# Values of six attention units computed two units at a time, in a one-core cross-attention block

## The chip, the cores and the metric

The kernel runs on one NeuronCore of a Trainium2 chip. The core has five engines that run at the same time and meet only at semaphores: TensorE (PE, the matrix array; PEld is its weight load), VectorE (DVE), ScalarE (ACT), GpSimd (POOL) and SyncE (SP), which here only issues transfers. Matrix products land in PSUM, eight banks of 128 x 512 float32; everything else lies in SBUF. The metric is the device time of one execution, the median of several runs. All data is float32.

## The reference, cut to what matters

Four sequences (batch `B = 4`) of 512 tokens with 512 channels each attend, with 16 heads of 32 channels, to 512 context tokens of their own; a two-layer MLP with 2048 hidden channels follows.

```python
x = layer_norm(hidden_states, ln1_w, ln1_b)
q = (x @ q_w + q_b);  k = (ctx @ k_w + k_b);  v = (ctx @ v_w + v_b)   # heads of 32
scores = einsum('bhqd,bhkd->bhqk', q, k) / sqrt(32), masked
out = softmax(scores) @ v
hidden = out @ cproj_w + cproj_b + hidden_states
y = gelu(layer_norm(hidden, ln2_w, ln2_b) @ fc_w + fc_b) @ proj_w + proj_b
return hidden + y
```

The change touches only the order in which parts of `q`, `k`, `v` and of the first layer norm are computed, and how the products for `v` are cut. No number of the reference is left out or changed.

## The kernel before, in words

**Units and blocks.** The attention is cut into 16 units, numbered `w`: batch `w // 4`, group `w % 4` of four heads (128 channels). Each unit has two halves of 256 queries, so there are 32 blocks, numbered `p = 2 w + half`; a half is also called a pair in the code. A block (`block`, L349) issues the scores of eight tiles (two query tiles by four heads, `scores`, L324), which fill all eight PSUM banks, then takes each score tile through VectorE (`soften`, L335: add the mask, take the minimum) and ScalarE (L339: exponential and row sum), turns the results by 32 x 32 blocks on VectorE (`turn`, L347), takes the reciprocal of the sums (L366), spreads it on ScalarE into `rr` (L368) and turns that too (L372). What comes out is the tile `tb`.

**Exchange.** The turned blocks must change partition groups. `exchange` and `copies` (L390, L397) move `tb` to a tile `pT` or `gt`: four diagonal pieces are copied by GpSimd (L405), twelve others go by transfers on SP's queue (L410). A pair's move is issued only when its target is free. Pairs 0, 2, 4, 6, 8 share the target `pT` and pairs 1, 3, 5, 7 the target `gt`, so that the move of pair 2 is issued when pair 0 has been attended, at the start of block 3.

**Attend.** `attend` (L415) multiplies the exchanged probabilities with the unit's `v` (L429) and scales the result on VectorE into `oT` (L434). In blocks 3 to 8 a block begins with the attend of the pair three blocks back, followed at once by the next exchange, if one waits: block 3 attends pair 0, block 4 pair 1, block 5 pair 2 and so on.

**Dense items.** Between the scores and the next attend TensorE does dense work from a list per block, `put(p, ...)`: `prep_k(w)` (L257), `prep_q(w)` (L267) and `prep_v(w)` (L279). Each makes one PSUM tile of 128 x 512. For K and Q the stationary operand is a weight block of 128 x 128 and the moving one has 512 columns. For V it is turned round: a token block of the context is stationary and the weight block of one unit, 128 columns, moves; 16 matmuls make a tile, in the profile 32 instructions at L285 (each float32 matmul is two). ScalarE copies the tile to `v` (L290) and GpSimd adds the bias (`v_bias`, L321). `prep_v_pair(w)` (L300) exists already and serves units 10 to 15: the two units' weight blocks, neighbours in SBUF, move together as 256 columns (L310); two PSUM tiles come out, each holding two token blocks of both units, so ScalarE makes four copies of 128 x 256 (L314). Each item ends by issuing on SP the load of a later unit's weights into the place it has read: K and Q of unit `w + 2` (up to unit 9), V of unit `w + 2`. Such a load waits until the item's matmuls are done, and SP is in order.

**Where an item lands.** Each entry of a list has a cost; `block` calls `fill(0)` after the last `soften`, `fill(1)` after the `rr` work and `fill(2)` after the call of `exchange`.

```python
def run(work, budget=None):
    spent = 0.0
    while work and (budget is None or spent + work[0][0] / 2 <= budget):
```

`fill(0)` and `fill(1)` have a budget of `CHAIN = 3.4`, the cost of one item, `fill(2)` has none. A `do(...)` entry costs 0.0 and goes with the item ahead of it; a `next_(...)` entry costs 0.01, does not fit behind an item, and goes to the next fill. A `V(w)` entry is a whole pair of units at the cost of one item. The order of issue is the order on each engine's queue: nothing is reordered later.

**Layer norm 1 of batch 1.** It is computed in the transposed layout: `load_raw(1)` (L200) loads the transposed input, `store_rn(1)` (L205) writes mean and scale per token to DRAM, `load_rn(1)` (L213) reads them back as two broadcast rows (tile `hid`), `ln1_rows` (L218) applies them on GpSimd, two operations of 128 x 512 for each of four chunks (L221), and `ln1_affine` (L223) applies weight and bias on ScalarE into `xT` (L225), which `prep_q(4)` reads. `load_enc(1)` (L180) loads batch 1's context over batch 0's, once unit 3's V has read it.

Of the kernel before, what the change touches and what calls it, by code (L numbers as in the profile page):

```python
# [25 lines left out]
ND = D // P  # L26
# [27 lines left out]
def xattn_block(ctx: ExitStack, tc: tile.TileContext, x, rawT, encT, mask, q_w, k_w, v_w, c_w, fc_w, p_w, vecs, rows, out):  # L54
# [41 lines left out]
    def k_q(w, i):  # L96
        n = w % 4 * 2 + i
        return pbt[:, n * D : (n + 1) * D]
# [23 lines left out]
    def acc_tile(name):  # L122
        n = count[5]
        count[5] += len(banks) > 1
        return banks[n // 4 % len(banks)].tile([P, D], F32, tag="acc", name=name)
# [51 lines left out]
    def queue(b):  # L177
        return Q[0] if b else nc.sync

    def load_enc(b):  # L180
        for d in range(ND):
            queue(b).dma_start(out=eT[:, d, :], in_=encT[b, ts(d, P), :])
# [17 lines left out]
    def load_raw(b):  # L200
        S["xn", b] = [tiles.tile([P, L], F32, tag="xn", name=f"raw_{b}_{d}") for d in range(ND)]
        for d in range(ND):
            nc.sync.dma_start(out=S["xn", b][d], in_=rawT[b, ts(d, P), :])

    def store_rn(b):  # L205
        nc.vector.transpose(rnT, rn)
        d = S["rn", b] = dram.tile([2, L], F32, tag=f"rn{b}", name=f"rn{b}")
        for i in range(NI):
            nc.sync.dma_start(
                out=d.rearrange("a (t i q) -> i (a t) q", i=NI, q=HD)[i], in_=rnT[i * HD : i * HD + 2 * NT, :]  # L210
            )

    def load_rn(b):  # L213
        S["rows", b] = [hid2[:, i] for i in range(2)]
        for i in range(2):
            nc.sync.dma_start(out=S["rows", b][i], in_=S["rn", b][i : i + 1, :].broadcast_to([P, L]))

    def ln1_rows(b, *ds):  # L218
        for d in ds:
            for i, op in enumerate((ALU.mult, ALU.add)):  # L220
                nc.gpsimd.tensor_tensor(S["xn", b][d], S["xn", b][d], S["rows", b][i], op)  # L221

    def ln1_affine(b):  # L223
        for d in range(ND):
            nc.scalar.activation(  # L225
                xT[:, d, :], S["xn", b][d], AF.Identity,
                bias=vec[:, LN1B + d : LN1B + d + 1], scale=vec[:, LN1W + d : LN1W + d + 1],
            )
# [14 lines left out]
    def load_w(w, queue=None, names=("wk", "wq", "wv")):  # L243

        if w >= NW:
            return
        g = w % NG
        for i, (n, src) in enumerate((("wk", k_w), ("wq", q_w), ("wv", v_w))):
            if n in names:
                S[n, w] = kqv_w(w, i)  # L250
                (queue or Q[0]).dma_start(out=S[n, w], in_=src[:, g, :, :])

    def next_w(w, name):
        if w != SINGLE - 1:
            load_w(w + (2 if w < SINGLE else 1), names=(name,))
# [11 lines left out]
    def prep_q(w):  # L267
        b, g = divmod(w, NG)
        qT = k_q(w, 1)
        parts = [slice(0, L)] if w else [slice(0, 2 * P), slice(2 * P, L)]  # L270
        for c in parts:
            acc = acc_tile(f"accq_{w}_{c.start}")[:, c]
            for d in range(ND):
                nc.tensor.matmul(acc, S["wq", w][:, d, :], xT[:, d, c], start=(d == 0), stop=(d == ND - 1))  # L274
            nc.scalar.activation(qT[:, c], acc, AF.Identity, bias=qb[:, g : g + 1], scale=-scale)
        next_w(w, "wq")
        S["qT", w] = qT

    def prep_v(w):  # L279
        b = w // NG  # L280
        v = five.tile([P, NT, P], F32, tag="v", name=f"v_{w}")
        acc = acc_tile(f"accv_{w}")
        for t in range(NT):
            for d in range(ND):
                nc.tensor.matmul(  # L285
                    acc[:, ts(t, P)], eT[:, d, ts(t, P)], S["wv", w][:, d, :],
                    start=(d == 0), stop=(d == ND - 1),
                )
        load_w(w + 2, names=("wv",))
        nc.scalar.copy(v, acc.rearrange("p (t f) -> p t f", t=NT))  # L290
        S["v", w] = v
        if w:
            v_bias(w)
# [6 lines left out]
    def prep_v_pair(w, later=False):  # L300
        pair = range(w, w + 2)
        for u in pair:
            S["v", u] = five.tile([P, NT, P], F32, tag="v", name=f"v_{u}")
        n = 10
        wv = ptt[:, n * D : (n + 2) * D].rearrange("p (g d f) -> p d g f", g=2, d=ND)
        for i in range(2):
            acc = acc_tile(f"accv_{w}_{i}").rearrange("p (t g f) -> p t g f", t=2, g=2)
            for t in range(2):
                for d in range(ND):
                    nc.tensor.matmul(  # L310
                        acc[:, t], eT[:, d, ts(2 * i + t, P)], wv[:, d], start=(d == 0), stop=(d == ND - 1)
                    )
            for g, u in enumerate(pair):
                nc.scalar.copy(S["v", u][:, 2 * i : 2 * i + 2], acc[:, :, g])  # L314
        for u in pair:
            load_w(u + 2, names=("wv",))
            (held_back.append if later else run_)(lambda u=u: v_bias(u))

    def v_bias(w):
        v, bias = S["v", w], row[:, 2, ts(w % NG, P)]  # L320
        nc.gpsimd.tensor_tensor(v, v, bias[:, None, :].broadcast_to([P, NT, P]), ALU.add)  # L321
# [141 lines left out]
    def c_bias(b):  # L463
        for t in range(NT):
            add_row(S["h", b, t], 0)
# [650 lines left out]
    CHAIN, TURN = 3.4, 0.5  # L1116

    def do(fn):
        return [(0.0, fn)]

    def next_(fn):
        return [(0.01, fn)]

    def A(w):
        if w >= NW:
            return []
        return [
            (CHAIN, lambda: prep_k(w)),
            (CHAIN, lambda: prep_q(w)),
            (CHAIN, lambda: prep_v(w)),  # L1130
        ]

    def V(w, later=False):
        return [(CHAIN, lambda: prep_v_pair(w, later))]

    def C(b):
        return [(CHAIN, lambda t=t: cproj(b, t)) for t in range(NT)]
# [4 lines left out]
    def turns2(b):  # L1142
        return [(TURN, lambda d=d: ln2_turn(b, d)) for d in range(ND)]

    def inputs(b):
        ln = [(0.0, lambda part=part: ln1(b, part)) for part in range(3)]
        return do(lambda: load_x(b)), ln, turns1(b), do(lambda: load_enc(b))
# [70 lines left out]
    def cb(b):  # L1218
        return do(lambda: c_bias(b))
# [7 lines left out]
    def stat(b, *ts_):  # L1227
        return do(lambda: [stat2(b, t) for t in ts_])
# [6 lines left out]
    def put(p, *work, before=(), mid=()):  # L1235

        work = [item for part in work for item in part]
        ahead[p], mids[p] = list(before), list(mid)
        fills[p] = work

    k2, q2, v2 = A(2)
    k3, q3, v3 = A(3)
    k4, q4, v4 = A(4)
    k5, q5, v5 = A(5)
    k6, q6, v6 = A(6)
    put(0, [(CHAIN, lambda: prep_v(1)), v2], do(lambda: (load_raw(1), store_rn(1))), [k2])
    put(1, [k3, (0.0, lambda: prep_q(1)), (CHAIN, lambda: (prep_v(3), load_enc(1)))], next_(lambda: load_rn(1)))
    put(2, [q2], [q3], do(lambda: ln1_rows(1, 0, 1)))
    put(3, [k4], do(lambda: ln1_rows(1, 2, 3)), [v4])
    put(4, [k5, v5], do(lambda: ln1_affine(1)))  # L1250
    put(5, [q4, q5])
    put(6, [k6, q6])
    x1, x2, x3, x4 = inputs(2)
    k, q, v = A(7)
    c, t2 = C(0), turns2(0)
    put(7, [v6, k], cb(0))
    put(8, x1, [q, v], x4)
    put(9, c[:1], do(lambda: attend(3, 1)), x2[:2], c[1:2], x2[2:], stat(0, 0), c[2:3], stat(0, 1),
        c[3:], stat(0, 2), x3, stat(0, 3), rs(0))
    k, q, v = A(8)  # L1260
    put(10, [k], norm(0, 0, 1), [v], norm(0, 2, 3), do(fc_sums), [q], t2)
    k, q, v = A(9)
    put(11, [k, v], some(2), pb_(0), mid=do(lambda: y_sums(0)))

    x1, x2, x3, x4 = inputs(3)
    put(12, [q], some(2))
    k, q, v = A(10)
# [4 lines left out]
    k, q, v = A(11)  # L1272
    put(16, do(lambda: ln1_rows(3, *range(ND))), [k, q], some(2), h_(1, 0, 1))
    put(17, next_(lambda: ln1_affine(3)), h_(1, 2, 3), x4, cb(1), C(1))
    k, q, v = A(12)
    put(18, [q], some(2), pre(0, 1))
    k12 = k
    k, q, v = A(13)
# [3 lines left out]
    k, q, v = A(14)  # L1282
# [100 lines left out]
```

## Time and profile before

| | |
|---|---|
| Time, median of 3 runs | 755.8 us (755.66 to 756.85) |
| The profiled execution | 756.21 us, its span 754.4 us |
| TensorE busy | 749.5 us, 99% of the span |
| VectorE busy | 617.5 us, 82% |
| GpSimd busy | 403.6 us, 53% |
| ScalarE busy | 341.1 us, 45% |

The span is the part of the execution that the profiler's records cover; 1.8 us lie around it. A busy share is a mean over stages; the change lies in the first 125 us, where the attention is densest. The chain of work that ended last is read backwards from the end of the kernel: whoever is on it sets the time.

### The profile page before, as it was taken

Reading aid. Unit: us, or ns where it says so; the run is one execution under the profiler, and the core shown is the slowest. Engines: PE = TensorE matmul, PEld = TensorE weight load, DVE = VectorE, ACT = ScalarE, POOL = GpSimd, SP = SyncE. Lnnn points to the kernel's source line nnn. Section 1 sums busy time; section 2 is a strip of 40 time slices with the busy share of each in tenths; the row PEclk is TensorE's granted clock in tenths of the full one; section 3 lists DMA queues with packets and bytes.
Section 4 is the critical chain, followed back from the end, with each engine's and each line's share of the span. In section 5 each row is a group of like instructions: output and inputs, shape, how many; then the busy total and the mean of one; then the engine's idle time right before and its main releaser. Section 6 shows DMA issues by size and latency. Waiting matters only on the chain.

```text
span 754.4 us, 13326 instructions
## 1 busy us (share of the span) xinstructions
PE 749.5 (99%) x4514; PEld 536.4 (71%) x4514; DVE 617.5 (82%) x1225; ACT 341.1 (45%) x776; POOL 403.6 (53%) x401
## 2 busy tenths in 40 slices
PE   9999999999999999999999999999999999999998
PEld 6655555467667546575655776468888899988998
DVE  3889999879998779877987999949877986957865
ACT  2566776555884575648853578401302221021200
POOL 1436838358597987667869974532150014403153
PEclk9999999999999999999999999999999999999999
DMA  9988888466787797666756757766734402045001
GB/s 327 342 240 238 227 216 248 116 182 188 216 240 233 210 258 188 165 191 160 196 127 202 192 145 240 185 216 236 242 104 151 156 15 91 29 157 207 1 15 43
DMA packets 61124, 134.62 MB, mean 178 GB/s; under 512 B 11344, under 2 KB 17360, under 8 KB 60928
## 3 DMA queue, kind: packets, MB, share of 16 engines
q1 hardware_dynamic: 58736, 127.39, 58.7%
q0 software_dynamic: 1600, 5.97, 2.5%
q8 instruction: 36, 0.59, 0.3%
q10 hardware_dynamic: 720, 0.41, 0.2%
q14 instruction: 32, 0.26, 0.1%
HBM read 69.23 MB, written 11.02 MB: 106 GB/s over the span
## 4 chain that ended last, share of the span: by engine, by line
PE 99%; DVE 0%; issue 0%; POOL 0%; POOLq 0%; DVEq 0%
PE q L671 26%; PE r L912 10%; PE sc L329 9%; PE av L429 8%; PE acck L262 8%; PE accq L274 7%; PE accc L471 6%; PE accv L285 5%; PE accp L766 4%; PE accv L310 3%; PE q1p L979 2%; PE tp L169 1%; PE q1j L785 1%; PE q3j L785 1%; PE q4j L785 1%; PE q6j L785 1%
## 5 line engine op out<-in xcount | busy, mean ns | idle before, releaser
L339 ACT ACTIVATE ptt<-ptt,mn 128x512 f32<-128x512 f32 x256 | 181.7, 711 | 140.2 <-DVE mn L335 140.2
L335 DVE CUSTOM_DVE_ANT_0 ptt<-sc,mb 128x512 f32<-128x512 f32 x256 | 160.6, 682 | 19.3 <-PE sc L329 19.3
L347 DVE STREAM_TRANSPOSE tb<-ptt 128x1024 f32<-128x1024 f32 x128 | 153.3, 1217 | 0.0
L405 POOL COPY pT<-tb 32x1088 f32<-32x1088 f32 x96 | 104.6, 1090 | 33.4 <-DVE oT L434 13.5
L671 PE MATMUL q<-yT,gt 128*128 128x256 f32 x320 | 78.9, 379 | 0.0
L692 ACT ACTIVATE ga<-ga,vec 128x512 f32<-128x512 f32 x40 | 26.7, 714 | 90.7 <-DVE ga L625 90.7
L329 PE MATMUL sc<-pbt 32*128 32x512 f32 x512 | 66.6, 615 | 0.0
L671 PEld LDWEIGHTS q<-yT,gt 128*128 128x128 f32 x320 | 60.7, 190 | 8.2
L671 PE MATMUL q<-ys,gt 128*128 128x256 f32 x240 | 61.6, 379 | 0.0
L262 PE MATMUL acck<-xe,ptt 128*128 128x512 f32 x128 | 59.7, 610 | 0.0
L274 PE MATMUL accq<-xe,ptt 128*128 128x512 f32 (+1 forms) x136 | 58.1, 573 | 0.0
L671 PEld LDWEIGHTS q<-ys,gt 128*128 128x128 f32 x240 | 45.6, 190 | 6.2
L625 DVE TENSOR_TENSOR ga<-q,ga 128x512 f32<-128x512 f32 (+1 forms) x60 | 36.2, 603 | 14.7 <-PE q L671 11.7
L339 ACT ACTIVATION_READ_ACCUMULATOR ptt<-ptt,mn 128x1 f32 x256 | 47.8, 187 | 0.0
L440 POOL TENSOR_TENSOR hid<-hid,row 128x512 f32<-128x512 f32 x18 | 24.0, 1359 | 42.7 <-DMA hid<-xa 42.6
L274 PEld LDWEIGHTS accq<-xe,ptt 128*128 128x128 f32 x136 | 25.0, 190 | 30.4 <-issue 23.0
L429 PE MATMUL av<-pT,v 128*32 128x256 f32 x768 | 46.4, 382 | 0.0
L262 PEld LDWEIGHTS acck<-xe,ptt 128*128 128x128 f32 x128 | 23.6, 194 | 31.9 <-issue 23.5
L329 PEld LDWEIGHTS sc<-pbt 32*128 32x128 f32 x512 | 27.5, 183 | 25.6 <-issue 16.9
L471 PE MATMUL accc<-wc,oT 128*128 128x512 f32 x96 | 42.5, 597 | 0.0
L285 PEld LDWEIGHTS accv<-ptt,xe 128*128 128x128 f32 x320 | 37.0, 192 | 4.9 <-DVE mn L335 2.7
L321 POOL TENSOR_TENSOR v<-v,row 128x512 f32<-128x512 f32 x16 | 20.3, 1278 | 37.2 <-ACT v L290 29.7
(263 smaller groups left out, 1436.8 us busy)
## 6 DMA issues: line engine op xcount, KB each, us to landing
pT<-tb SPq DMA_DIRECT2D x288, 136.0 KB
pbt<-p_w_dram SPq DMA_DIRECT2D x40, 256.0 KB
gt<-ws SPq DMA_DIRECT2D x20, 512.0 KB
gt<-tb SPq DMA_DIRECT2D x48, 136.0 KB
xe<-tb SPq DMA_DIRECT2D x48, 136.0 KB
pbt<-fc_w_dram SPq DMA_DIRECT2D x24, 256.0 KB
gt<-fc_w_dram SPq DMA_DIRECT2D x20, 256.0 KB
ptt<-k_w_dram SPq DMA_DIRECT2D x16, 256.0 KB
```

The lines of the kernel that those rows point to most:

```text
L262: nc.tensor.matmul(acc, S["wk", w][:, d, :], eT[:, d, :], start=(d == 0), stop=(d == ND - 1))
L274: nc.tensor.matmul(acc, S["wq", w][:, d, :], xT[:, d, c], start=(d == 0), stop=(d == ND - 1))
L285: nc.tensor.matmul(acc[:, ts(t, P)], eT[:, d, ts(t, P)], S["wv", w][:, d, :], start=(d == 0), stop=(d == ND - 1),)
L329: nc.tensor.matmul(S["sc", w, qt][h], qT[r, ts(qt, P)], kT[r, :], start=True, stop=True)
L335: nc.vector.tensor_tensor_reduce(out=s, in0=S["sc", w, qt][h], in1=S["mb", w // NG], scale=1.0, scalar=FMAX, op0=ALU.add, op1=ALU.min, acc ...
L339: nc.scalar.activation(s, s, AF.Exp, bias=mn, scale=-1.0, accum_out=S["sums", w][:, qt, h : h + 1])
L347: nc.vector.transpose(tv[:, qt % 2, 2 * k : 2 * k + 2], S["ps", w, qt, k])
L405: nc.gpsimd.tensor_copy(pT[ts(i, HD), i], tb[ts(i, HD), i])
L429: nc.tensor.matmul(av[ts(h, HD), : 2 * P].rearrange(shape, **kw), v[:, t, ts(h, HD)], p[t][h], start=(t == 0), stop=(t == NT - 1),)
L471: nc.tensor.matmul(acc, S["oT", b][:, g, ts(t, P)], wc[:, g, :], start=(g == 0), stop=(g == NG - 1))
L671: nc.tensor.matmul(o, x[:, k], y[:, k], start=(k == 0), stop=(k == 1))
L912: nc.tensor.matmul(r, x[:, c], w[:, c], start=(c == 0), stop=(c == NP // 2 - 1))
```

## The change

The lists of blocks 0 to 8 are written anew. V of units 2 and 3, of 4 and 5 and of 6 and 7 is made by `prep_v_pair`, in blocks 1, 4 and 8, in place of six single `prep_v` in blocks 0, 1, 3, 4, 7 and 8. K of units 3, 5 and Q of unit 7 move one block earlier into the freed places (K of unit 2 from the third to the second place of block 0). `ln1_rows(1)`, GpSimd's part of batch 1's layer norm 1, is issued whole at the end of block 2, where before half of it stood in block 2 and half in block 3; `ln1_affine(1)` stays in block 4, now in `fill(1)` without an item ahead of it.

```diff
-    put(0, [(CHAIN, lambda: prep_v(1)), v2], do(lambda: (load_raw(1), store_rn(1))), [k2])
-    put(1, [k3, (0.0, lambda: prep_q(1)), (CHAIN, lambda: (prep_v(3), load_enc(1)))], next_(lambda: load_rn(1)))
-    put(2, [q2], [q3], do(lambda: ln1_rows(1, 0, 1)))
-    put(3, [k4], do(lambda: ln1_rows(1, 2, 3)), [v4])
-    put(4, [k5, v5], do(lambda: ln1_affine(1)))
+    put(0, [(CHAIN, lambda: prep_v(1)), k2], do(lambda: (load_raw(1), store_rn(1))), [k3])
+    put(1, [(CHAIN, lambda: prep_q(1))], V(2), do(lambda: load_enc(1)), next_(lambda: load_rn(1)))
+    put(2, [q2], [q3], next_(lambda: ln1_rows(1, *range(ND))))
+    put(3, [k4], [k5])
+    put(4, V(4), next_(lambda: ln1_affine(1)))
     put(5, [q4, q5])
     put(6, [k6, q6])
     x1, x2, x3, x4 = inputs(2)
     k, q, v = A(7)
     c, t2 = C(0), turns2(0)
-    put(7, [v6, k], cb(0))
-    put(8, x1, [q, v], x4)
+    put(7, [k, q], cb(0))
+    put(8, x1, V(6), x4)
```

The function that the new lists call, unchanged by the diff:

```python
def prep_v_pair(w, later=False):
    pair = range(w, w + 2)
    ...
    for i in range(2):
        acc = acc_tile(f"accv_{w}_{i}").rearrange("p (t g f) -> p t g f", t=2, g=2)
        for t in range(2):
            for d in range(ND):
                nc.tensor.matmul(
                    acc[:, t], eT[:, d, ts(2 * i + t, P)], wv[:, d], start=(d == 0), stop=(d == ND - 1)
                )
        for g, u in enumerate(pair):
            nc.scalar.copy(S["v", u][:, 2 * i : 2 * i + 2], acc[:, :, g])
    for u in pair:
        load_w(u + 2, names=("wv",))
        (held_back.append if later else run_)(lambda u=u: v_bias(u))
```

## The prediction

> **What bounds the kernel now.** I read the page's head and its chain first, then the chain in order of time for the stretch that the change touches, then each other engine's timeline there.
>
> ```profile
> span 754.4 us, 13326 instructions
> PE 99%; DVE 0%; issue 0%; POOL 0%; POOLq 0%; DVEq 0%
> ```
>
> The chain never leaves TensorE: a microsecond taken from its list is taken from the end, unless a wait comes up. The chain in order of time (start, length, what; blocks 0, 1, 3, 4, 7, 8 in turn, then a pair of V, then two rows of later blocks):
>
> ```profile
> 24.22 7.34 PE accv L285 x64
> 31.57 3.44 PE acck L262 x8
> ...
> 36.93 3.63 PE acck L262 x8
> 40.56 3.43 PE accq L274 x8
> 43.99 3.57 PE accv L285 x32
> ...
> 60.35 3.63 PE acck L262 x8
> 63.98 3.57 PE accv L285 x32
> ...
> 71.35 3.63 PE acck L262 x8
> 74.98 3.57 PE accv L285 x32
> 78.55 1.86 PE av L429 x32
> 80.41 1.93 PE sc L329 x16
> ...
> 104.10 3.77 PE accv L285 x32
> 107.87 3.44 PE acck L262 x8
> ...
> 115.13 3.63 PE accq L274 x8
> 118.76 3.57 PE accv L285 x32
> ...
> 226.89 6.91 PE accv L310 x32
> ```
>
> ```profile
> 323.39 7.10 PE accv L310 x32
> ...
> 442.28 2.97 PE sc L329 x16
> ```
>
> The reader is to see that the pieces abut (71.35 + 3.63 = 74.98, + 3.57 = 78.55), so TensorE waits nowhere here, and that an item right behind scores costs 0.2 more than one behind another item: 3.63 against 3.43, 3.77 against 3.57, 7.10 against 6.91. VectorE, from block 4 into block 5:
>
> ```profile
> 80.02 0.40 DVE L372 STREAM_TRANSPOSE tb<-rr 128x256 f32<-128x256 f32 x1
> 80.48 0.42 DVE L434 TENSOR_TENSOR oT<-av,pT 128x256 f32<-128x256 f32 x1
> 81.50 0.69 DVE L335 CUSTOM_DVE_ANT_0 ptt<-sc,mb 128x512 f32<-128x512 f32 x1 [0.60 <-PE sc L329]
> ```
>
> VectorE ends a block only just when TensorE does (80.42 against 80.41) and then idles 0.60 until the first score tiles are there, 1.09 behind the start of the scores. That 0.60 is all its slack per block: the second engine near the bound.
>
> **The change, TensorE.** Each V pair replaces two singles; the rest is regrouped. By the rows above, dense time per block, before and after:
> - Block 0: 7.34 + 3.44 = 10.78; then V1, K2, K3 = 3.77 + 3.44 + 3.44 = 10.65. -0.13.
> - Block 1: 3.63 + 3.43 + 3.57 = 10.63; then Q1 and the pair, 3.63 + 6.91 = 10.54. -0.09.
> - Block 3: 7.20; then K4, K5 = 3.63 + 3.44. -0.13.
> - Block 4: 7.20; then the pair behind scores, 7.10. -0.10.
> - Block 7: 3.77 + 3.44 = 7.21; then K7, Q7 = 3.63 + 3.43 = 7.06. -0.15.
> - Block 8: 7.20; then 7.10. -0.10.
>
> Sum -0.70, of which -0.45 has come by the start of block 5. It is little because a single's instruction with 128 moving columns takes 3.57 / 32 = 111.6 ns and a pair's with 256 takes 6.91 / 32 = 215.9: two against one save 7.3 ns, 32 times for each of three pairs, 0.70.
>
> The Trainium skill ("TensorE: Matmul & The Clock Gate", section "Wait — 56ns, not 53.3ns?") puts the fixed cost of a matmul at about 2.5 ns beyond its columns. By that, three times 32 fewer would save 0.24, or 0.48 if each of these float32 instructions is two passes, and the sum would start from there; the rows here say 7.3 ns, and I go by the rows.
>
> **ScalarE and VectorE.** Rows of ScalarE at the end of block 4, and four copies of an existing pair:
>
> ```profile
> 78.60 0.67 ACT L264 ACTIVATE pbt<-acck,vec 128x512 f32<-128x512 f32 x1
> 79.17 0.39 ACT L368 COPY rr<-rsum 128x256 f32<-128x256 f32 x1
> ...
> 79.94 2.94 ACT L225 ACTIVATE xe<-raw,vec 128x512 f32<-128x512 f32 x4
> ```
>
> ```profile
> 330.64 1.17 ACT L314 COPY v<-accv 128x256 f32<-128x256 f32 x4
> ```
>
> In blocks 4 and 8 the whole pair stands in the first fill, so four copies (1.17) stand ahead of `rr` where one eviction (79.17 - 78.60 = 0.57) stood; the second tile's copies also wait for TensorE, whose pair ends in block 4 at 71.35 - 0.35 + 7.10 = 78.10, before ScalarE gets there (78.60 - 0.35 = 78.25). What is queued behind that new wait is `rr`, the affine and the next block's exponentials. `rr` starts at 78.25 + 1.17 = 79.42 and ends 79.81; VectorE would take it up at 80.02 - 0.35 = 79.67. So VectorE ends the block 0.15 to 0.3 later than its own shift, out of a slack of 0.60 of which the shorter block uses 0.10. I cost it at nothing; bounds 0 and 0.3 in each of two blocks if that slack is not what it seems. The affine starts 0.15 earlier to 0.2 later than 79.94; its first of four chunks (0.74) is needed by Q4 at 82.34 - 0.45 = 81.89, over a second later. PSUM sees no change: a pair takes two tiles, like two items.
>
> **GpSimd and the transfers.** The one place where the cover is thin. GpSimd's rows from block 1 to 4, and SP's:
>
> ```profile
> 49.54 4.47 POOL L405 COPY gt<-tb 32x1088 f32<-32x1088 f32 x4
> 62.80 5.22 POOL L221 TENSOR_TENSOR raw<-raw,hid 128x512 f32<-128x512 f32 x4 [8.79 <-DMA hid<-rn]
> 67.97 4.47 POOL L405 COPY pT<-tb 32x1088 f32<-32x1088 f32 x4
> 72.52 5.22 POOL L221 TENSOR_TENSOR raw<-raw,hid 128x512 f32<-128x512 f32 x4
> ```
>
> ```profile
> 47.60 0.33 SPq L251 DMA_DIRECT2D ptt<-v_w_dram  x1
> 47.98 1.84 SPq L182 DMA_DIRECT2D xe<-encT_dram  x4
> 49.93 8.87 SPq L410 DMA_DIRECT2D gt<-tb  x12
> 58.84 1.08 SPq L216 DMA_DIRECT2D hid<-rn  x2
> ```
>
> GpSimd waits until 62.80 for the two broadcast rows, applies half of them, and only then makes pair 2's copies (67.97 to 72.44), because block 2's call of `exchange` finds `pT` held and the copies are issued in block 3. After the change all eight operations stand in block 2's list and so ahead of these copies: 67.97 - 62.80 = 5.17 more. The copies end at 72.44 + 5.17 = 77.61 plus whatever the rows come later. Block 5 needs them at 78.55 - 0.45 = 78.10. A cover of 6.1 becomes one of 0.49.
>
> How much later do the rows come? On SP the order ahead of them is unchanged but for one V load (unit 4's), which moves from block 0 to behind V's last matmul in block 1; unit 4's K load takes its place, unit 5's K load stays ahead. SP's gate opens 0.22 earlier and one more issue costs 47.98 - 47.60 = 0.38: +0.16 if issue alone counts. If the sixteen transfer engines are full, 256 KB more go ahead:
>
> ```profile
> 47.60:52.00 4.40, 4.40 (x22) 2.04 (x23) 3.35 (x11) 3.20 (x8) 3.58 (x4) 1.00 0.76 264
> 52.00:56.00 4.00, 4.00 (x11) 1.71 (x9) 4.00 (x9) 2.41 (x8) 1.97 (x2) 1.00 1.06 278
> ```
>
> ```profile
> ptt<-v_w_dram SPq DMA_DIRECT2D x16, 256.0 KB
> ```
>
> The last two columns are the transfer engines' share and GB/s: 24% idle at first, then full. 0.262 MB at 264 GB/s is 0.99, less 0.22: +0.77. I take +0.45, the middle, since half of the stretch has idle room. The copies then end at 78.06, the wait is 0 to 0.4 between the two ends, and I cost it at 0.1, mostly the passing of the semaphore.
>
> The Trainium skill ("DMA: Bandwidth & Descriptors", section "Specifications") gives about 358 GB/s to a core from HBM; by that the 256 KB are an estimated 0.73 us, and the wait would be about 0.1 as well. The trace shows 264 and 278 where the engines are busy.
>
> The other moves have one answer. The biases of V2 and V3 put 1.28 more ahead of pair 1's copies (49.54 to 54.01, needed at 63.98 + 3.57 = 67.55, cover 13; without it 1.3). K5's, K7's, Q7's weight loads and V6's to V9's keep their order against the exchange transfers or move by one place among 0.4 us issues; SP reaches them later than their matmuls end, so the new waits hold up nothing. The context load of batch 1 is gated by the end of block 1's dense work as before, 0.22 earlier. The affine has all rows sooner. Batch 0's `cproj` bias no longer waits behind V6's bias on GpSimd; V6's bias goes to block 8, where its unit isn't attended before block 9's list.
>
> **Sum.** -0.70 + 0.1 = -0.6. The profiled execution took 756.21, 1.8 outside its span, and is 0.4 above the median of 755.8; a difference of 0.6 is carried to the median as it is: 755.2. Two tenths of a per cent, 1.5 us, is about what a measurement of this kernel can tell from no change, and the three runs shown spread by 1.2. So: no change that can be told, with a small gain most likely.
>
> **The rivals.**
> - Late copies (mild). Pair 1's twelve transfers took 8.87 to issue; a similar set later takes 7.76:
>
> ```profile
> 91.84 7.76 SPq L410 DMA_DIRECT2D gt<-tb  x12
> ```
>
>  so 1.1 of back-pressure stood there already. If the extra load adds that much again, the rows come 0.16 + 1.1 = 1.3 later, TensorE waits 0.9 at block 5's attend, and the kernel takes 756.0. The span between is 755.5 to 756.3. Chance 0.22.
> - Late copies (severe), the other side. The same wait decides from rows 1.2 later on (0.49 + 0.70): from there the kernel is slower; slower by over 1.5 needs them 2.7 late. For it: everything on GpSimd is in order, and rows, rows, copies, attend is now one chain without slack. Against: no bound above gives more than 1.3. Time 757.5. Chance 0.10.
> - VectorE becomes the bound: its slack of 0.60 is gone in blocks 4 and 8 because `rr` comes late; 0.3 lost twice, 755.8. Against: the working above leaves it 0.2 to 0.4. Chance 0.08.
> - The change does less than the rows say, with the saving at 0.24 (the smaller fixed cost): 755.7. Against: singles and pairs are measured here in the same program. Chance 0.04.
> - More than the sum: the scores at 442.28 take 2.97 where others take 1.93, a wait of 1.04, and there are smaller ones; shifted work could lose them, 753.9. Against: VectorE's and GpSimd's work there shifts with TensorE. Chance 0.07.
> - The forecast, copies in time or nearly: 755.0 to 755.5. Chance 0.49.
>
> **The numbers.** The likeliest is 755.2. The range leaves out the severe case and the one with more than the sum (0.17): from the forecast's low end, 755.1, and the mild case's high end, 756.3, each widened by half the spread of the runs, 0.6: 754.5 to 756.9. Faster by over 0.2% is the last-but-one case and a little of the forecast's scatter, 0.09; slower is the severe case and some of the mild one's scatter, 0.13; the rest, 0.78, is within.
>
> **What would show it.** In the chain: pairs of 6.91, 7.10 and 7.10 in blocks 1, 4, 8, and block 5's scores at about 79.9 to 80.1 instead of 80.41. On GpSimd: eight operations of L221 in one run from about 63.2, pair 2's copies behind them to about 78. A wait of `av` on GpSimd's copy in block 5 beyond half a microsecond, rows landing after 64, or VectorE's first minimum of blocks 5 and 9 without an idle stretch ahead of it would show me wrong.

## The result, and the profile after

The changed kernel takes 763.55 us (median of 6 runs, 762.04 to 765.22); the kernel before took 755.73 beside it (755.14 to 758.15). The ratio is 1.0098, with a 95% interval of 1.0076 to 1.012: 7.8 us slower, where 755.2 was predicted and 756.9 was the top of the range. The profiled execution took 765.22, its span is 763.4, 9.0 longer than before.

The chain of the page still names TensorE first, but no longer alone, and one of the costliest groups has a wait that it did not have:

```profile
span 763.4 us, 13144 instructions
PE 94%; DMA 2%; POOL 2%; DVE 1%; issue 1%; ACT 0%; SPq 0%; DVEq 0%; POOLq 0%
L347 DVE STREAM_TRANSPOSE tb<-ptt 128x1024 f32<-128x1024 f32 x128 | 153.4, 1217 | 5.6 <-POOL pT L405 5.5
```

The third line is the group to begin with: the turns on VectorE (L347) were kept idle for 5.5 us, and what ended it was a GpSimd copy into `pT`. The chain in order of time shows the place (start, length, what):

```profile
70.62 2.52 POOL raw L221 x2
...
74.43 1.08 POOL pT L405
...
77.81 1.10 POOL pT L405
78.94 1.30 DVE tb L347 x2
...
81.23 0.65 DVE ptt L335
81.93 1.52 ACT ptt L339 x4
83.45 0.54 ACT v L314 x2
84.03 3.71 PE sc L329 x6
87.74 8.99 PE accq L274 x16
```

It runs from GpSimd's layer norm rows through pair 2's four copies to VectorE's first turn of block 4, from there through ScalarE to block 5's scores. No link in it is the attend of pair 2, which the prediction had taken as the reader of these copies. The engines' timelines in that stretch, GpSimd, VectorE, TensorE of the kernel after (start, length, engine, line, operation, count; in brackets the idle time before and who ended it):

```profile
64.10 10.39 POOL L221 TENSOR_TENSOR raw<-raw,hid 128x512 f32<-128x512 f32 x8 [9.79 <-DMA hid<-rn]
74.43 4.47 POOL L405 COPY pT<-tb 32x1088 f32<-32x1088 f32 x4
```

```profile
78.94 2.37 DVE L347 STREAM_TRANSPOSE tb<-ptt 128x1024 f32<-128x1024 f32 x2 [5.53 <-POOL pT L405]
```

```profile
78.95 1.93 PE L429 MATMUL av<-pT,v 128*32 128x256 f32 x32 [1.36 <-POOL pT L405]
80.82 2.87 PE L329 MATMUL sc<-pbt 32*128 32x512 f32 x10
84.03 3.71 PE L329 MATMUL sc<-pbt 32*128 32x512 f32 x6 [0.35 <-ACT v L314]
87.67 9.06 PE L274 MATMUL accq<-xe,ptt 128*128 128x512 f32 x16
96.66 1.93 PE L429 MATMUL av<-gt,v 128*32 128x256 f32 x32
```

And the same turn, the same scores and the dense items behind them before:

```profile
74.18 2.37 DVE L347 STREAM_TRANSPOSE tb<-ptt 128x1024 f32<-128x1024 f32 x2
```

```profile
80.34 2.00 PE L329 MATMUL sc<-pbt 32*128 32x512 f32 x16
82.35 7.11 PE L274 MATMUL accq<-xe,ptt 128*128 128x512 f32 x16
89.38 1.93 PE L429 MATMUL av<-gt,v 128*32 128x256 f32 x32
```

The reader is to see who waits for the copies. They read pair 2's `tb` and write `pT`. The attend of pair 2 reads `pT`; it waited 1.36. But `tb` has two buffers (`two.tile(..., tag="tb")` in `block`, L354), used in turn by the pairs: pair 4, which block 4 makes, writes into the buffer that pair 2 had. So VectorE's first `turn` of block 4 may not start before the last of the four copies has read it. Before the change it came at 74.18, 1.74 after the copies had ended at 72.44. Now the copies end at 78.9 and VectorE stands still until 78.94, with the last two softened tiles of the block behind it; ScalarE, in order, waits 7.21 for the next minimum, and its evictions and the score banks of block 5 come late. Block 5's scores, 2.01 long before (80.34 to 82.35), take 6.85 (80.82 to 87.67).

On top of that TensorE was slowed. The stretches of 4 us (busy time and count of PE, PEld, DVE, ACT, POOL; then the granted clock, the transfers' share, GB/s), after and then before:

```profile
76.00:80.00 4.00, 2.64 (x28) 1.74 (x30) 1.06 (x1) 0.00 (x0) 3.86 (x4) 1.00 0.88 207
80.00:84.00 4.00, 3.68 (x30) 1.15 (x18) 4.00 (x9) 2.07 (x7) 3.31 (x4) 1.00 0.83 240
84.00:88.00 4.00, 3.97 (x7) 1.49 (x8) 4.00 (x12) 4.00 (x8) 3.56 (x4) 0.59 0.32 73
88.00:92.00 4.00, 4.00 (x6) 1.67 (x6) 3.94 (x9) 3.88 (x12) 3.23 (x3) 0.55 0.85 201
92.00:96.00 4.00, 4.00 (x11) 1.75 (x10) 3.62 (x8) 2.39 (x6) 0.00 (x0) 1.00 0.85 219
```

```profile
84.00:88.00 4.00, 4.00 (x10) 1.71 (x9) 4.00 (x9) 3.11 (x10) 3.92 (x4) 1.00 0.99 228
```

The granted clock is 0.59 and 0.55 in the two stretches from 84 to 92. These are means: in stretches of half a microsecond it is 0.50 from 85.0 to 91.5, and the trace's own record has 0.50 from 84.75 to 91.58, 6.83 us. The two Q items take 8.99 (87.67 to 96.66) instead of 7.03 (82.35 to 89.38): 3.91 of them lie in the time at half clock, and half of that is the difference of 1.96. PE is shown as busy all through, from 88 to 92 with 6 matmuls, all of the Q items, where the kernel before has 10 of the same items in 4 us: a busy share doesn't show a slow clock.

The loss can be added up on TensorE. I compare the start of each attend with the kernel before. Pair 2's stands at +0.47, its wait of 1.36 in it; the scores of block 5 add 4.84, the Q items 1.96: 7.27, and pair 3's attend is measured at +7.28. The last of these scores lie in the time at half clock as well; how much of the 4.84 is the clock's isn't separated here. All six runs have a mean granted clock below 1 (0.995 to 0.998). From pair 4 on the offset shrinks, to +7.04 at pair 6, and stays there up to block 17. There this trace loses another 2.67:

```profile
267.25 1.93 PE L429 MATMUL av<-pT,v 128*32 128x256 f32 x32 [2.60 <-POOL raw L221]
```

This is the attend of pair 15. SP's queue of the kernel after, and that before, show why it is late:

```profile
248.62 1.30 SPq L209 DMA_DIRECT2D rn<-rnT  x4
253.79 0.82 SPq L216 DMA_DIRECT2D hid<-rn  x2
254.72 7.83 SPq L410 DMA_DIRECT2D pT<-tb  x12
```

```profile
241.58 1.31 SPq L209 DMA_DIRECT2D rn<-rnT  x4
245.25 0.82 SPq L216 DMA_DIRECT2D hid<-rn  x2
246.17 8.52 SPq L410 DMA_DIRECT2D pT<-tb  x12
```

The store of batch 3's row statistics has to land before they are loaded again: the gap is 253.79 - 249.92 = 3.87 instead of 245.25 - 242.89 = 2.36, and pair 15's twelve transfers stand behind the load in the queue. The diff doesn't touch this code, and e2 below loses as much as the changed kernel without this second wait (its offset is +8.20 at pair 14 and at pair 16), so the median's 7.8 doesn't need it. Whether it is scatter or comes with the pairs isn't shown. Of the traces that load these rows on SP, the three without pairs (before, e2, e9) have gaps of 2.36, 2.18 and 2.22; the five with pairs (changed, e1, e3, e4, e8) have 3.87, 3.65, 2.57, 2.36 and 4.56.

### The profile page after: what moved, and what is told of

Same layout as the page of the kernel before. It is cut to its first block, busy times and chain, and to the rows that moved or that the text cites. A ratio compares the mean times of both kernels' runs of the same rounds, so it can differ in the third digit from the quotient of the medians.

```text
span 763.4 us, 13144 instructions
## 1 busy us (share of the span) xinstructions
PE 754.5 (99%) x4418; PEld 534.2 (70%) x4418; DVE 618.0 (81%) x1225; ACT 341.6 (45%) x782; POOL 403.6 (53%) x401
## 4 chain that ended last, share of the span: by engine, by line
PE 94%; DMA 2%; POOL 2%; DVE 1%; issue 1%; ACT 0%; SPq 0%; DVEq 0%; POOLq 0%
PE q L671 25%; PE r L912 10%; PE sc L329 8%; PE accq L274 7%; PE av L429 7%; PE acck L262 6%; PE accc L471 6%; PE accv L310 5%; PE accp L766 4%; PE q1p L979 2%; PE accv L285 2%; PE tp L169 1%; POOL raw L221 1%; PE q1j L785 1%; PE q3j L785 1%; PE q4j L785 1%
## 5 line engine op out<-in xcount | busy, mean ns | idle before, releaser
L347 DVE STREAM_TRANSPOSE tb<-ptt 128x1024 f32<-128x1024 f32 x128 | 153.4, 1217 | 5.6 <-POOL pT L405 5.5
L671 PE MATMUL q<-yT,gt 128*128 128x256 f32 x320 | 78.9, 379 | 0.0
L329 PE MATMUL sc<-pbt 32*128 32x512 f32 x512 | 70.7, 619 | 0.3 <-ACT v L314 0.3
L274 PE MATMUL accq<-xe,ptt 128*128 128x512 f32 (+1 forms) x136 | 60.0, 589 | 0.0
L310 PE MATMUL accv<-ptt,xe 128*128 128x256 f32 x192 | 42.7, 381 | 0.0
```

The lines of the kernel that those rows point to most:

```text
L310: nc.tensor.matmul(acc[:, t], eT[:, d, ts(2 * i + t, P)], wv[:, d], start=(d == 0), stop=(d == ND - 1))
L329: nc.tensor.matmul(S["sc", w, qt][h], qT[r, ts(qt, P)], kT[r, :], start=True, stop=True)
L347: nc.vector.transpose(tv[:, qt % 2, 2 * k : 2 * k + 2], S["ps", w, qt, k])
L671: nc.tensor.matmul(o, x[:, k], y[:, k], start=(k == 0), stop=(k == 1))
```

## The experiments

The theory after the first comparison: the whole loss is the move of the eight operations ahead of pair 2's copies, and it comes through VectorE's turn into the same buffer. Its rivals: the loss comes through late `pT` and the attend (the prediction's own worry, at a larger size); or the regrouped loads and pairs cause it.

**e1: the change with the rows split as before.** V in pairs, but half of the eight operations again behind pair 2's copies:

```diff
-    put(2, [q2], [q3], next_(lambda: ln1_rows(1, *range(ND))))
-    put(3, [k4], [k5])
+    put(2, [q2], [q3], do(lambda: ln1_rows(1, 0, 1)))
+    put(3, [k4], do(lambda: ln1_rows(1, 2, 3)), [k5])
```

> The V pairs and the regrouped items are kept; only GpSimd's part of the layer norm is put back (four operations in block 2, four in block 3 behind pair 2's copies). Buffer theory (VectorE's first turn of block 4 writes the tile out of which pair 2's copies read, since there are two such tiles, so these copies are due at about 73.5 and not at block 5's attend): with four operations ahead the copies end at about 64 + 5.2 + 4.5 = 73.8, a wait within VectorE's slack of 0.6; the kernel takes the forecast -0.7 against before, about 755.0. Attend theory (the one of the prediction: copies due at 78.1): the same, 755.0. Pair theory (four ScalarE copies ahead of rr, or the moved weight loads, cost the time): still 7 to 8 slower than before.

Measured: 756.6 (754.98 to 760.46, 12 runs) beside 756.12, ratio 1.0007, 95% interval 0.9992 to 1.0022. GpSimd and VectorE of e1:

```profile
68.37 4.47 POOL L405 COPY pT<-tb 32x1088 f32<-32x1088 f32 x4
```

```profile
72.91 2.37 DVE L347 STREAM_TRANSPOSE tb<-ptt 128x1024 f32<-128x1024 f32 x2
```

The copies end at 72.84 and the turn follows with no wait. All of the loss is gone with the pairs still in: they don't cause it. The gain that was expected on top, 755.0, doesn't show.

**e2: the rows alone.** The kernel before, and all eight operations in block 2's list:

```diff
-    put(2, [q2], [q3], do(lambda: ln1_rows(1, 0, 1)))
-    put(3, [k4], do(lambda: ln1_rows(1, 2, 3)), [v4])
+    put(2, [q2], [q3], next_(lambda: ln1_rows(1, *range(ND))))
+    put(3, [k4], [v4])
```

> The kernel before with the layer norm's eight operations in block 2 and no V pair. Buffer theory: rows land at 62.8 as before, copies end at 62.8 + 10.4 + 4.5 = 77.7, VectorE's turn due at 74.2 waits 3.5, of which 0.6 is slack: 2.9 lost at least, more if TensorE's granted clock falls as it did in the changed kernel (0.55 to 0.59 over 8 us, some 2 us): 758.6 to 761. Attend theory: copies at 77.7 are in time for 78.5, no change, 755.7. Pair theory: no change, 755.7.

Measured: 763.8 (760.96 to 764.28, 4 runs), ratio 1.0095, interval 1.0075 to 1.0114: the changed kernel's loss, in full, and above the 758.6 to 761 that the buffer theory had given with rows at 62.8. GpSimd, VectorE and the stretches of e2:

```profile
64.82 1.28 POOL L221 TENSOR_TENSOR raw<-raw,hid 128x512 f32<-128x512 f32 x1 [10.80 <-DMA hid<-rn]
```

```profile
79.83 2.37 DVE L347 STREAM_TRANSPOSE tb<-ptt 128x1024 f32<-128x1024 f32 x2 [5.56 <-POOL pT L405]
```

```profile
84.00:88.00 4.00, 3.60 (x8) 1.22 (x6) 4.00 (x10) 4.00 (x9) 3.69 (x4) 0.73 0.17 45
88.00:92.00 4.00, 4.00 (x5) 1.51 (x5) 3.90 (x10) 4.00 (x12) 3.40 (x4) 0.50 0.95 219
```

The same wait, and the same fall of the clock (0.50 from 85.84, again for 6.83 us). One more thing: the order of SP's loads here is that of the kernel before, and yet the rows landed at 64.82, later than in the changed kernel (64.10) and 2.0 later than before (62.80). So the load order, from which the prediction took its +0.45, doesn't by itself explain when the rows land. e1 has the changed order and starts on them at 62.27 (its second operation then waits 1.01 more, for the other row).

**e3: six of the eight ahead of the copies.** From the changed kernel:

```diff
-    put(2, [q2], [q3], next_(lambda: ln1_rows(1, *range(ND))))
-    put(3, [k4], [k5])
+    put(2, [q2], [q3], next_(lambda: ln1_rows(1, 0, 1, 2)))
+    put(3, [k4], do(lambda: ln1_rows(1, 3)), [k5])
```

> The changed kernel with six of the eight operations in block 2 and two in block 3 behind pair 2's copies. Buffer theory: copies end 2.6 earlier than in the changed kernel, at about 76.3, VectorE waits 2.9 instead of 5.5, 2.3 lost and 0.7 gained: 757.4, up to 759.5 if the clock falls too. Attend theory: 76.3 is in time for 77.6, 755.0. Pair theory: 762 to 763 as the changed kernel.

Measured: 760.08 (758.61 to 762.89, 4 runs), ratio 1.0066, interval 1.0044 to 1.0088. VectorE and TensorE of e3:

```profile
76.16 2.37 DVE L347 STREAM_TRANSPOSE tb<-ptt 128x1024 f32<-128x1024 f32 x2 [2.65 <-POOL pT L405]
```

```profile
77.63 1.93 PE L429 MATMUL av<-pT,v 128*32 128x256 f32 x32
79.50 4.52 PE L329 MATMUL sc<-pbt 32*128 32x512 f32 x16
83.94 7.13 PE L274 MATMUL accq<-xe,ptt 128*128 128x512 f32 x16
```

This run tells the two ways apart. The copies end at 76.1, ahead of the attend, which starts at 77.63 with no wait; the turn waits 2.65 all the same, and block 5's scores take 4.44 instead of 2.01 (79.50 to 83.94). Two operations fewer, 2.6 of GpSimd's time, take 2.9 off the turn's wait. The attend goes from -0.85 (pair 2) to +1.63 (pair 3) against the kernel before: 2.43 by the scores, and the rest 0.05. The buffer's next writer sets the time; its reader was early. In this trace the clock also stays at 1.00 in every stretch from 76 to 96. It is the shortest of the four runs, 758.61; the other three, at 759.97, 760.20 and 762.89, have mean granted clocks of 0.998, 0.998 and 0.995. So the median's loss of 4.0, more than the 757.4 to 759.5 expected, is the trace's 2.5 and, in those runs, lost clock too.

**e4: all eight behind the copies.** From the changed kernel, the rows in block 3's list:

```diff
-    put(2, [q2], [q3], next_(lambda: ln1_rows(1, *range(ND))))
-    put(3, [k4], [k5])
+    put(2, [q2], [q3])
+    put(3, [k4], do(lambda: ln1_rows(1, *range(ND))), [k5])
```

> The changed kernel with all eight operations in block 3, behind pair 2's copies. Buffer theory: pair 2's copies no longer wait for the rows at all and run from about 58 to 62.5; the operations end at about 74.5, in time for the affine at about 79.5; pair 3's copies come behind them, 74.5 to 79, due at block 5's first turn at about 84.5: no wait, 755.0. Attend theory: 755.0. Pair theory: 762 to 763.

Measured: 756.44 (755.28 to 761.25, 12 runs), ratio 1.0014, interval 0.9997 to 1.003. The copies, no longer behind the load of the rows, run from 58.10 to 62.5, ten microseconds ahead of the turn, which has no wait at 73.26. With e1 this makes a scale: eight operations ahead of the copies, a wait of 5.5; six, 2.65; four or none, none. The pairs' gain is in the trace but not in the time, which the last six runs followed up.

**Where the pairs' gain goes: e5 to e10.** In e1's trace the attends stand ahead of the kernel before by 1.18 (pair 0), then 1.42 and, behind blocks 7 and 8, 1.66; this holds to pair 14 at 240 us. At pair 15 the lead turns into +0.40, and from pair 17 on it is 0.00. In e4 it is 1.35 to pair 14, 1.13 at pair 15 and 0.06 from pair 17 on. Not all of this is the pairs': at block 0's first score, ahead of all that was changed, e1 is already 0.95 ahead and e4 0.64, and e9 below, without pairs, 1.18. TensorE of e1 at pair 15, and of e4 at block 18's scores and the items behind:

```profile
257.94 1.93 PE L429 MATMUL av<-pT,v 128*32 128x256 f32 x32 [1.98 <-DMA pT<-tb]
```

```profile
276.00 3.51 PE L329 MATMUL sc<-pbt 32*128 32x512 f32 x16
279.44 3.70 PE L274 MATMUL accq<-xe,ptt 128*128 128x512 f32 x8
```

Two places take the lead back: in e1 pair 15's transfers, behind the round trip of the row statistics; in e4 block 18's scores, which wait for PSUM banks held by batch 1's `cproj`, whose addition waits for GpSimd's bias on the tiles `h`, which waits for their load. In e4's chain in order of time these links stand:

```profile
269.31 5.33 DMA h<-x_dram
...
274.76 0.56 POOL h L440
...
277.31 0.70 DVE h L472
...
278.06 1.45 PE sc L329 x4
```

That load doesn't land earlier when TensorE does: e4's affine starts 1.13 earlier than that of the kernel before (267.52 against 268.65), and its last addition on VectorE starts at 277.31, against 277.36. Block 18's scores end at 279.4 to 279.6 in e1, e4 and the kernel before alike; in e1, already 0.40 behind, they don't wait (2.00 long), in the kernel before they take 2.43.

e5 moves the load of batch 3's rows from SP's queue to GpSimd's (on top of e4), e6 does the same to the kernel before, e7 moves it to ScalarE's queue (on top of e4):

```diff
-            nc.sync.dma_start(out=S["rows", b][i], in_=S["rn", b][i : i + 1, :].broadcast_to([P, L]))
+            (nc.gpsimd if b == 3 else nc.sync).dma_start(out=S["rows", b][i], in_=S["rn", b][i : i + 1, :].broadcast_to([P, L]))
```

In e7 `nc.scalar` stands in place of `nc.gpsimd`.

> The kernel with all eight operations in block 3, and batch 3's two broadcast rows loaded from GpSimd's queue instead of SP's, so that pair 15's twelve transfers no longer stand behind the round trip of the row store (2.4 to 3.9 in the profiles so far). Theory of the eaten gain: the 0.7 of the pairs, whole until block 16 in both kernels without the stall, is lost at block 17's attend, which waits for these transfers; here the wait goes and 755.4 or less against 756.1 is seen. If it is lost elsewhere (the residual loads ahead of block 18's scores), no change against before. If the pairs cost something outside the profile, no change either.

> The kernel before with the same change of queue for batch 3's rows and no V pair. Theory of the eaten gain: before's own profile has no wait at block 17, so 0 to 0.5 faster, with fewer slow runs; the kernel with pairs and this change stays 0.5 to 0.7 ahead of this one. If the waits behind block 17 set the time, both are equal.

> As the kernel with the rows loaded from GpSimd's queue, but from ScalarE's, which is idle for 4.2 ahead of block 16's exponentials. Theory of the eaten gain: as that one, 755.4 or less, unless a late row store holds the exponentials (up to 1.5), 756. If the time is set behind block 17: no change against before.

Measured: e5 760.13, ratio 1.0057 (1.0039 to 1.0075); e6 761.02, ratio 1.0064 (1.0044 to 1.0084); e7 756.47, ratio 1.0008 (0.9999 to 1.0017). Pair 15 is in time in all three, but from GpSimd's queue it costs more than it brings. GpSimd and TensorE of e5:

```profile
245.40 1.18 POOL L216 DMA_DIRECT2D hid<-rn  x2 [2.94 <-DMA rn<-rnT]
```

```profile
278.76 1.72 PE L329 MATMUL sc<-pbt 32*128 32x512 f32 x4 [0.83 <-DVE hid L472]
```

The wait for the store now stands in GpSimd's own order, everything behind it is late, and the chain of bias, addition and scores at block 18 loses some 6 in the traces: pair 17's attend is at +5.96 in e5 and +5.95 in e6. Part of that is again the clock, at 0.50 for 6.83 us from 280.92 in e5 and for 3.41 us from 283.38 in e6: the Q item behind the scores takes 5.77 and 4.84 instead of 3.54. That e6, without pairs, loses as much shows that the change of queue does this, and not the pairs. In e7 the lead survives pair 15 (0.66 at pair 16) and goes at block 18 (0.12 at pair 17).

e8, e9 and e10 therefore issue the load of the `h` tiles earlier, from ScalarE's queue, in the middle of the affine of batch 3 (e8 on top of e4, e9 on the kernel before, e10 on top of e7; `ln1_affine` takes chunk numbers for this, as `ln1_rows` does):

```diff
-    put(17, next_(lambda: ln1_affine(3)), h_(1, 2, 3), x4, cb(1), C(1))
+    def affine_h():
+        ln1_affine(3, 0, 1)
+        Q[0] = nc.scalar
+        load_h(1, 2, 3)
+        Q[0] = nc.sync
+        ln1_affine(3, 2, 3)
+
+    put(17, next_(affine_h), x4, cb(1), C(1))
```

> The kernel with pairs and all eight operations in block 3; in block 17 the two late tiles of batch 1's residual input are loaded from ScalarE's queue after half of the affine, not from SP's behind pair 16's twelve transfers. Clamp theory (the pairs' gain is whole until block 16 and lost at block 18's scores, which wait for PSUM tiles of the output projection, whose additions wait for GpSimd's bias on these tiles, 274.6 to 276 in the profiles): they land about 1.3 earlier, the wait shrinks by as much, and 0.5 to 0.7 is kept: 755.2 against 755.9. If the gain is eaten by something else, equal to before.

> The same change of queue on the kernel before, without pairs. Clamp theory: its own profile loses 0.4 at block 18's scores, so 0.2 to 0.4 faster, and 0.5 behind the kernel that has the pairs too. Otherwise no change.

> Pairs, all eight operations in block 3, batch 3's rows from ScalarE's queue and the two residual tiles from ScalarE's queue: both places behind block 16 where profiles showed the gain going. Clamp theory: 755.0 or less, the best of the three. Otherwise equal to before.

Measured, beside 756.1 for the kernel before: e8 756.57, ratio 1.0016 (1.0001 to 1.0031); e9 756.23, ratio 1.0005 (0.9994 to 1.0016); e10 756.29, ratio 1.0007 (0.9994 to 1.0019). In two of the three traces this does what it should: e9 takes block 18's wait away (its lead grows from 1.18 to 1.58 there), and e10 keeps a lead of 1.57 to pair 15 and 1.21 to the end (0.86 of it from before block 0's scores), in an execution of 755.05. In the medians no gain can be told, and e8's interval lies just above 1: e10's twelve runs lie between 754.94 and 759.09, the kernel before's between 754.9 and 757.95. e8's traced run, the longest of its twelve at 762.01, shows other waits: VectorE's turn of block 4 waited 2.70, the release put down to the load of a K weight, and the attend of pair 15 waited 2.92 for its transfers. VectorE and TensorE of e8:

```profile
76.33 2.37 DVE L347 STREAM_TRANSPOSE tb<-ptt 128x1024 f32<-128x1024 f32 x2 [2.70 <-DMA ptt<-k_w_dram]
```

```profile
262.08 3.00 PE L429 MATMUL av<-pT,v 128*32 128x256 f32 x32 [2.92 <-DMA pT<-tb]
```

No kernel tried is measurably faster than the kernel before; the 755.0 to 755.4 expected of e1, e4, e5, e7, e8 and e10 didn't come.

## Why the prediction was wrong

The step that failed is the sentence "Block 5 needs them at 78.55 - 0.45 = 78.10. A cover of 6.1 becomes one of 0.49." The deadline of pair 2's copies is not their reader, the attend of block 5, but the next writer of the buffer that they read: VectorE's first turn of block 4, at 74.18 before. The true cover was 74.18 - 72.44 = 1.74. Moving 5.17 of work ahead of the copies overdraws it by 3.4 even if the rows come no later. The row of that turn lay in the VectorE timeline of the kernel before; the prediction shows that timeline only from 80.02 on, and takes the reader of the copies' result for the only one whom they can hold up. Two of its own signs of being wrong came with the changed kernel: `av` waited 1.36 for GpSimd's copy, and the rows landed after 64.

The other points, in its order:

- **TensorE, -0.70: right.** e1's pair 0 is attended 1.18 ahead of the kernel before. The regrouped blocks 0 and 1 make 0.23 of that (0.22 was worked out); 0.95 stood already before them. From pair 6 on the lead is 1.65 or 1.66: 0.70 of it by the change. In the changed kernel, too, the offset falls by 0.24 from pair 4 to pair 6, where -0.25 was worked out for blocks 7 and 8, and the chain has pairs of 6.91 and 7.10 as forecast. What was wrong is "carried to the median as it is": the lead is taken back at blocks 17 and 18, by transfers and a load that don't follow TensorE. The rival "More than the sum" looked at such waits and took them for room to gain.
- **ScalarE and VectorE, nothing: not contradicted.** In e4, where the copies are in time, the first minimum of block 5 still has 0.46 of idle time ahead of it, where 0.60 stood; the working had left 0.2 to 0.4.
- **GpSimd's eight operations: the size right, the landing wrong.** They took 10.39 in one run (10.44 by the rows). The rows landed 1.30 later than before in the changed kernel, outside the bounds of 0.16 to 0.77. Over e1 to e4 and the changed kernel the first operation starts at 62.27, 64.82, 63.91, 63.49 and 64.10, and the latest of these is e2, whose load order is that of the kernel before: the landing scatters by 2 or more, and a bound taken from one trace was no bound. The attend's wait of 1.36 is what the rival of late copies (mild) had priced at 0.9; it is the small part of the loss.
- **The severe rival** had the sign and part of the place, the copies behind the rows; its price, 757.5, lacked the turn.
- **PSUM sees no change: so for the pairs** (e1, e4). In the changed kernel the banks of block 5 come free late, but as a result of the turn.
- **The clock** was not thought of. Of the 7.28, the two Q items took 1.96 more at a granted clock of 0.50, which the prediction, by counting a stall at its own length, could not have.

What stays open: what makes the pair kernels' runs, with up to 0.70 less work on TensorE, spread upwards as far as 761 (e4) and 762 (e8). Two things on record narrow it. First, most of the longest runs have a lower mean granted clock: 0.998, 0.998 and 0.995 in e4's 759.22, 760.49 and 761.25 (0.999 or 1.000 in its other nine), 0.997 and 0.998 in e10's longest three and in e8's 759.34 and 762.01; but e8's 759.23 and 758.49 have 1.000. Second, `tb` has other readers than the copies: the twelve transfers of the same pair on SP. In e5, which loses 0.94 between pair 2's and pair 3's attend, block 4's first turn waits for pair 2's:

```profile
73.59 2.37 DVE L347 STREAM_TRANSPOSE tb<-ptt 128x1024 f32<-128x1024 f32 x2 [1.11 <-DMA pT<-tb]
```

e8's trace loses 2.53 there, behind the wait of 2.70 at the same turn. The profile names the K weight's load, which stands right behind these transfers in SP's queue; they were issued until 73.20, later than in every other trace (70.0 to 71.7), so they may be what the turn waited for. The lead brings the turn forward, to 73.26 in e4 from 74.18, and the transfers don't follow (issued until 71.27 in e4, 70.45 before). That this sets the spread isn't shown. e1 and e4 lose nothing there, some traces lose more at pairs 15 to 17, and the other runs have no trace. A third buffer for `tb`, which would take the turn's wait away with the rows left in place, was not tried.

## What to carry to other kernels

When work is put ahead of an operation on an in-order engine, find two deadlines: who reads what it writes, and who next writes the buffer that it reads. In a ring of two buffers the second can come first, as here by 4.4 us (74.18 against 78.55), and it stands in the code only as the number of buffers of a tile. And a gain on the engine that bounds the kernel is worth only as much as the loads and row exchanges further down let through: follow the start of one repeated step, pair by pair, over the whole trace, to see where a lead is lost.

## What the hardware showed that was not expected

**A stall can cost more than its length.** Behind a stretch with TensorE busy for 2.64 of 4 us (2.71 in e2) the granted clock was 0.50 for 6.83 us, and sixteen matmuls took 8.99 instead of 7.03. It began 5.8 us behind the end of the wait itself (78.95), at 84.75, when TensorE was issuing again; in e2 6.0 behind it. e5 has such a fall of 6.83 and e6 and e8 one of 3.41, each behind or within waits. But the idle times of 2.60 and 1.98 ahead of pair 15's attend, in the changed kernel and in e1, have none behind them, nor has e3's trace, where block 5's scores were spread over 4.44. The Trainium skill ("TensorE: Matmul & The Clock Gate", section "Part 1: The HAM clock gate") gives half the clock after at least one idle window of some 3.4 us. The traces agree with the half, 0.50; but in the changed kernel the fall came without an idle time as long as that window: the longest shown are 1.36 and 0.35, with thinly spaced scores between.

**The transfers' landing scatters by more than the gains at stake.** The row statistics' way through DRAM (store of four, then the load) took from 2.18 us (e2) to 4.56 (e8) with the same code, and the first row of batch 1 was ready anywhere from 61.32 (e9) to 65.19 (e8). Where an in-order queue has work behind such a round trip, this goes straight into the time: 2.60 at pair 15's attend, or, in GpSimd's queue, a wait of 2.94 that became some 6 in e5's trace, the lost clock included, and 4.3 in its median.
